# Six pairs of turned inputs put behind each other in a fused three-attention and MLP kernel

## The chip, the cores and the metric

The kernel runs on one core of a Trainium2 chip (trn2). The metric is the device time of one execution in microseconds (us); the figure for a kernel is the median of several executions. A profile is a separate, traced execution of the same program; it gives a span, from the first to the last instruction, and its own execution time beside it.

## The reference, cut to what matters

The input is `x` with 16 batches of 256 tokens and 256 features, and a context `y` of the same shape. Each batch goes through three attentions of 16 heads of 16 features, one after the other, and then through an MLP. All is float32.

```python
# layer 0: cross attention, RMS norms
q = rmsnorm(x) @ Wq;  k, v = rmsnorm(y) @ Wk, rmsnorm(y) @ Wv
x = rmsnorm(x + attention(q, k, v) @ Wo)
# layer 1: causal self attention with a layer norm ahead and rotary q and k
h = layernorm(x);  q, k, v = h @ sa_wq, h @ sa_wk, h @ sa_wv
x = x + causal_attention(rope(q), rope(k), v) @ sa_wo + sa_bo
# layer 2: cross attention with a layer norm ahead and rotary q and k
h = layernorm(x);  q = h @ ca_wq;  k, v = y @ ca_wk, y @ ca_wv
x = x + attention(rope(q), rope(k), v) @ ca_wo + ca_bo
# MLP
x = x + gelu(layernorm(x) @ fc1 + b1) @ fc2 + b2
```

The layers of one batch depend on each other. Different batches do not.

## The kernel before, in words

There are 48 attentions, three for each of 16 batches. Their order is written out by hand in the string `ORDER`, one digit for the layer of each; the n-th 0, the n-th 1 and the n-th 2 belong to batch n. The loop over `i` has 48 steps; step `i` does the scores and the values of attention `i`, and between them pieces of its neighbours. Within each engine the instructions stand in the order in which this loop names them; a manual schedule keeps it.

A step of layer 0 or layer 2 has four blocks `n` = 0 to 3. A step of layer 1, the causal one, has three, since one quarter of the scores is masked. In each block TensorE (PE in the profile) does scores (L472), values of the block before (L511), and then one dense product of 16 groups of rows:

- block 0: `q` of attention `i + 1` (L290)
- block 1: `k` of `i + 1` (L290)
- block `final - 1`: `v` of `i + 1` (L303); in a causal step this is block 1, so it follows `k` directly
- block `final`: the output projection `project` of `i - 2` (L303), and then the `turn` of `i + 2` (L270)

The turn makes the normalised input of an attention feature-major, since the products need it so. `turned` takes one PSUM bank, does four 128x128 transposes on TensorE (matmuls against the identity), and ScalarE (ACT) copies the bank to SBUF into a tile with the tag `hT` (L275). Attentions of layer 0 need no turn: their input is loaded in that layout already. So there are 32 turns.

What a turn needs is made by VectorE (DVE) and GpSimd (POOL) in two pieces. `stats` does `bn_stats` and `bn_aggr` for each half of the tokens (L252, L253), and then GpSimd adds epsilon (L234) and takes the power -1/2 (L235). `norm` waits for that and writes the normalised rows `xn`, one VectorE instruction for each half (L259). For attention `i + 2` both stand in step `i`, in block 0 or 1.

The rest of VectorE's queue matters for the steps below. After `q` and after `k` it does the rotary embedding (L402, L406, L422, L424 for `qm`, and L431, which writes `kT`). In block `final - 1` it inverts the softmax sums of `i - 1` (L553, L554), and adds the bias to `v` (L452, tile `va`), which releases the PSUM bank of `v`. In block `final` it adds the projected output to the rows (L576, in layer 0 L573 with two square sums L242). In block 0 of the next step it copies the values out of PSUM (L528, tile `av`). `divide` (L567) needs the inverted sums spread over partitions by a trip through DRAM (`inv<-hop`, issued by SP).

All dense products and the turns share three PSUM banks with the tag `d`, in rotation. Scores use two double banks, values one bank. The mask of a causal step is applied by GpSimd on the exponentials (L490). The scores of step `i` begin with `kT` and `qm` of attention `i`.

After the loop the MLP of eight groups of two batches follows, with its own turns (L657) and sums of inputs (`mix`). In the last step `mix` borrows two tiles of the tag `hT`.

Of the kernel before, what the change touches and what calls it, by code (L numbers as in the profile page):

```python
# [8 lines left out]
F32 = mybir.dt.float32  # L9
# [6 lines left out]
P = 128  # L16
B, S, D = 16, 256, 256
# [11 lines left out]
N_ATT = 3 * B  # L29

ORDER = [int(n) for n in "000001010102210210210121021012210101021212122222"]
# [14 lines left out]
def xattn_kernel(  # L46
# [25 lines left out]
    work = tc.alloc_tile_pool(name="work", bufs=2)  # L72
# [30 lines left out]
    def load(b):  # L103
        load_x(b)
        load_y(b)

    def load_w(t, aps, eng):
        at = 0
        for a in aps:
            m = a.shape[1]  # L110
            eng.dma_start(out=t[:, :, at : at + m], in_=a.rearrange("(k p) n -> p k n", p=P))
            at += m
# [41 lines left out]
    def dense_ps():  # L154
        return psD.tile([P, 512], F32, tag="d", name="d")
# [55 lines left out]
    def fold_v():  # L211
        ps = dense_ps()
        for k in range(KC):
            for j in range(0, P, 32):
                nc.tensor.matmul(
                    ps[j : j + 32, :D],
                    lhsT=vec[:, V_B1 + k : V_B1 + k + 1].to_broadcast([P, 32]),
                    rhs=sa_sb[:, k, 2 * D : 3 * D],
                    start=(k == 0), stop=(k == KC - 1), skip_group_check=True,
                )  # L220
        row = bias_sb[:, R_SAV : R_SAV + D]
        nc.vector.tensor_tensor(row, ps[:, :D], row, ALU.add)

    def fold_gain(w, cols, vcol, chunks=range(KC)):
        for k in chunks:
            nc.vector.tensor_scalar(
                w[:, k, cols], w[:, k, cols], vec[:, vcol + k : vcol + k + 1], None, ALU.mult
            )
# [36 lines left out]
    def turned(src, name, pool, tag, bufs):  # L265

        ps = dense_ps()
        for c in range(NC):
            for k in range(KC):
                nc.tensor.transpose(  # L270
                    ps[:, k * S + c * P : k * S + (c + 1) * P],
                    src[:, c, k * P : (k + 1) * P], ident,
                )
        t = pool.tile([P, KC, S], F32, tag=tag, name=name, bufs=bufs)
        nc.scalar.copy(t.rearrange("p k s -> p (k s)"), ps)  # L275
        return t
# [34 lines left out]
    class Att:  # L311
# [74 lines left out]
        def turn(self):  # L386
            if self.layer == 0:
                self.hT = xTs.pop(self.b)
            else:
                self.hT = turned(self.xn, "hT", work, "hT", 2)  # L390
            self.kvT = self.hT if self.layer == 1 else yTs[self.b]

        def rotated(self, ps, n):
# [192 lines left out]
    atts = {}  # L586

    def att(i):
        if 0 <= i < N_ATT:
            return atts.setdefault(i, Att(i))  # L590
        return None

    def do(i, *names):
        a = att(i)
        for name in names:
            if a is not None:
                getattr(a, name)()
# [37 lines left out]
    class Mlp:  # L635
# [24 lines left out]
                        )  # L660
                copy(self.hT[:, :, i, :], ps.rearrange("p (k s) -> p k s", s=S))

        def mix(self, tag="av"):

            b = self.hT
            if tag == "av":
                ts = self.pool.tile([P, 4, S], F32, tag=tag, name="ts")
                self.ts = [ts[:, i] for i in range(4)]
            else:
                pairs = [self.pool.tile([P, 2, S], F32, tag=tag, name="ts") for _ in range(2)]  # L670
                self.ts = [t[:, i] for t in pairs for i in range(2)]
            t1, t2, t3, t4 = self.ts
            for o, x, y in (
                (t1, b[:, 0, 1], b[:, 0, 0]), (t2, b[:, 1, 1], t1),
                (t3, b[:, 1, 1], b[:, 0, 1]), (t4, b[:, 1, 0], t2),
            ):
                nc.vector.tensor_tensor(o, x, y, ALU.subtract)
# [186 lines left out]
    mlps = [Mlp(g, work) for g in range(B // 2)]  # L864
    combined = combine()

    with tc.manual_schedule():
# [9 lines left out]
        load(3)  # L877
        load_w(sa_sb, sa, nc.sync)

        kept = {}  # L880
        for j in range(N_ATT):
            slot = next(i for i in range(max(j - 1, 0), N_ATT + 1) if (ORDER + [0])[i] != 1)
            kept.setdefault(slot, []).append(j)
        for i in range(N_ATT):
            a, last = att(i), att(i - 1)
            ahead = att(i + 3)
            if i > 1 and ahead is not None and ahead.layer == 0:
                load(ahead.b)

            finishing = i >= 3 and att(i - 3).layer == 0
            follows = (
                finishing and i + 2 < N_ATT
                and att(i + 2).layer == 1 and att(i + 2).b == att(i - 3).b
            )
            for n in range(len(a.blocks)):
                if n == 0 and a.causal and not finishing:
                    do(i + 2, "stats")
                a.scores(n)  # L900
                if n > 0:
                    a.values(n - 1)
                elif last is not None:
                    last.values(-1)
                final = len(a.blocks) - 1
                if n == 0:
                    if i == 0:
                        a.v()
                        do(1, "spread")
                    if not follows and (finishing or not a.causal):  # L910
                        do(i + 2, "stats")
                    do(i - 1, "end")
                    do(i - 3, "finish")
                    if follows:
                        do(i + 2, "stats")
                    if not finishing:
                        do(i + 2, "norm")
                    if i == N_ATT - 3:
                        mlps[0].stats()
                    if i == N_ATT - 2:  # L920
                        mlps[0].norm()
                    do(i - 2, "divide")
                    if i == N_ATT - 1:
                        mlps[0].turn(nc.vector.tensor_copy)
                        mlps[0].keep()
                    do(i + 1, "q")
                elif n == 1:
                    do(i + 1, "k")
                    if finishing:
                        do(i + 2, "norm")  # L930
                    for j in kept.get(i, ()):
                        att(j).keep()
                    if i == N_ATT - 1:
                        do(i - 2, "project")
                        mlps[1].norm()
                if n == final - 1:
                    do(i - 1, "invert")
                    do(i + 1, "v")
                    do(i + 2, "send")
                    if i == N_ATT - 2:  # L940
                        mlps[1].stats()
                    if i == N_ATT - 1:
                        mlps[0].up(2)
                        mlps[0].mix("hT")
                if n == final:
                    if i == N_ATT - 1:
                        mlps[1].turn(nc.vector.tensor_copy)
                    else:
                        do(i - 2, "project")
                    do(i + 2, "turn", "receive")  # L950
                if i == 0 and n == 0:
                    load(4)
                    nc.sync.dma_start(out=bias_sb, in_=rows.partition_broadcast(P))
                    nc.sync.dma_start(out=turn_sb, in_=turn)
                if i == 0 and n == 1:
                    load_w(ca_sb, ca, nc.sync)
                if i == 0 and n == 2:
                    load_w(fc1_sb, [fc1], nc.sync)
                if i == 1 and n == 0:
                    load_w(sao_sb, [sa_o], nc.sync)  # L960
                    load_w(cao_sb, [ca_o], nc.sync)
                if i == 1 and n == 2:
                    load_w(fc2_sb, [fc2], nc.sync)
                    nc.sync.dma_start(
                        out=rope_sb, in_=rope.rearrange("(c p) t d -> p c t d", p=P)
                    )
                if i == 1 and n == 3:
                    cols = fold_bias()
                    fold_v()
                if i == 2 and n == 3:  # L970
                    fold_gain(sa_sb, slice(0, 3 * D), V_G1)
                if i == 3 and n == 3:
                    fold_cols(cols)
                    fold_gain(ca_sb, slice(0, D), V_G2)
                if i in (6, 8) and n == 3:
                    fold_gain(fc1_sb, slice(0, FF), V_G3, [i // 8])
                if n == 1 and i > 8 and not a.causal:
                    next(combined, None)
# [72 lines left out]
    with tc.If(n_good < P):  # L1051
        with tc.tile_pool(name="gen", bufs=1) as gen, tc.tile_pool(
            name="gps", bufs=2, space=bass.MemoryType.PSUM
# [14 lines left out]
        with tc.tile_pool(name="late2", bufs=2) as late2, tc.tile_pool(  # L1068
            name="psL2", bufs=2, space=bass.MemoryType.PSUM
# [391 lines left out]
```

## Time and profile before

| what | value |
|---|---|
| median of 3 runs | 947.22 us (946.21 to 947.79) |
| profiled execution, own time | 945.63 us |
| profiled execution, span | 943.80 us |
| PE busy | 931.4 us, 99% of the span |
| DVE busy | 656.8 us, 70% |
| ACT busy | 546.8 us, 58% |
| POOL busy | 297.6 us, 32% |
| granted TensorE clock | 1.000 |

Of the 943.8 us, the first 60 load and begin, the stretch from 60 to 720 holds the steady part of the 48 steps, and the rest is the MLP. A matmul's row in the profile lasts longer than the distance to the next matmul, because matmuls are pipelined; so the time that a group of matmuls takes is read from the start of its first to the start of the next group, which is what the chain of work that ended last shows. Times in a timeline are counted from the start of the span.

### The profile page before, as it was taken

The page shows a single profiled execution, that of the slowest core. Times are in us where ns is not written, and L with a number is a line of the kernel's source. Part 1 is how long each engine was busy: PE and PEld are TensorE (multiplying, and loading weights), DVE is VectorE, ACT ScalarE, POOL GpSimd, SP SyncE. Part 2 cuts the span into 40 slices and gives each one's busy share as a digit, 9 for nine tenths or more (in the row PEclk, how much of TensorE's full clock was granted, in tenths as well). Part 3 has the DMA queues.
Part 4 walks back from the last instruction along what each step waited for, and adds up shares of the span by engine and source line. Part 5 has one row for each costly group of instructions (what it writes and reads, how often), then busy time and mean ns, then how long its engine had stood idle before and what let it go on. Part 6 is the DMA issues. An engine that isn't in the chain of part 4 may idle for free.

```text
span 943.8 us, 29943 instructions
## 1 busy us (share of the span) xinstructions
PE 931.4 (99%) x12374; PEld 550.1 (58%) x12374; DVE 656.8 (70%) x1438; ACT 546.8 (58%) x770; POOL 297.6 (32%) x501
## 2 busy tenths in 40 slices
PE   8999999999999999999999999999999999999997
PEld 3444455445454555455454554455444799999997
DVE  4348577876777677768766767888877576666663
ACT  3666556765666666756655666666666634444440
POOL 3122543424253454243423333344123021222200
PEclk9999999999999999999999999999999999999999
DMA  9541322213131131311232211111111100000001
GB/s 311 172 114 50 93 84 55 87 37 93 44 91 40 45 88 48 87 46 37 87 85 80 59 46 42 35 49 40 39 39 39 37 23 23 12 12 23 23 25 48
DMA packets 77994, 58.77 MB, mean 62 GB/s; under 512 B 25748, under 2 KB 76948, under 8 KB 77848
## 3 DMA queue, kind: packets, MB, share of 16 engines
q1 hardware_dynamic: 76616, 55.68, 20.7%
q8 instruction: 100, 1.64, 0.7%
q10 hardware_dynamic: 1232, 1.07, 0.4%
q14 instruction: 46, 0.38, 0.1%
HBM read 38.34 MB, written 5.79 MB: 47 GB/s over the span
## 4 chain that ended last, share of the span: by engine, by line
PE 87%; DMA 6%; DVE 4%; SPq 2%; issue 1%; POOL 0%; ACT 0%; ACTq 0%; DVEq 0%
PE S L472 17%; PE A L511 16%; PE d L303 15%; PE d L290 15%; PE upX L681 6%; PE A L779 5%; PE downZ L779 3%; PE upZ L681 3%; PE d L270 2%; PE d L779 2%; PE d L681 1%; DMA hop<-sums 1%; DMA sums<-hop 1%; DMA hop<-av 1%; DMA rq_hop<-pad 1%; PE d L657 1%
## 5 line engine op out<-in xcount | busy, mean ns | idle before, releaser
L483 ACT ACTIVATE pt<-S 128x1024 f32<-128x1024 f32 x224 | 217.3, 1022 | 121.0 <-PE S L472 121.0
L472 PE MATMUL S<-qm,kT 32*128 32x512 f32 (+1 forms) x1536 | 201.9, 600 | 1.0 <-ACT kT L433 0.7
L511 PE MATMUL A<-pt,va 128*32 128x256 f32 (+1 forms) x3072 | 188.9, 367 | 2.5 <-DVE av L528 2.5
L511 PEld LDWEIGHTS A<-pt,va 128*32 128x32 f32 x3072 | 80.2, 109 | 156.1 <-issue 106.3
L483 ACT ACTIVATE pt<-S,sy 128x1024 f32<-128x1024 f32 x128 | 135.7, 1111 | 47.5 <-PE S L472 45.1
L490 POOL TENSOR_SCALAR_AFFINE_SELECT pt<-pt 128x512 f32<-128x512 f32 x128 | 87.7, 702 | 61.3 <-ACT pt L483 60.8
L472 PEld LDWEIGHTS S<-qm,kT 32*128 32x128 f32 x1536 | 62.0, 183 | 66.6 <-issue 40.4
L398 ACT ACTIVATE a<-d,qk_bias 128x256 f32<-128x256 f32 x128 | 53.8, 471 | 53.8 <-PE d L290 43.9
L234 POOL TENSOR_SCALAR r_ln<-bmv 128x2 f32<-128x2 f32 x48 | 12.9, 268 | 224.4 <-DVE bmv L253 223.2
L279 POOL TENSOR_TENSOR cur<-cur,bias 128x512 f32<-128x512 f32 x48 | 64.2, 1343 | 55.5 <-DVE xn L259 55.5
L567 DVE TENSOR_TENSOR oT<-oT,inv 128x512 f32<-128x512 f32 x48 | 41.5, 864 | 30.5 <-DMA hop<-av 8.5
L290 PE MATMUL d<-hT,sa 128*32 128x256 f32 x1024 | 61.2, 379 | 0.0
L259 DVE TENSOR_SCALAR xn<-cur,bmv,r_ln 128x256 f32<-128x256 f32 x96 | 51.6, 585 | 1.4 <-POOL r_ln L235 0.8
L576 DVE TENSOR_TENSOR cur<-d,cur 128x512 f32<-128x512 f32 x32 | 22.0, 688 | 40.6 <-PE d L303 40.6
L406 DVE TENSOR_TENSOR a<-a,turn 128x512 f32<-128x512 f32 x64 | 48.1, 752 | 2.2
L417 DVE SCALAR_TENSOR_TENSOR qm<-d,vec,rq 128x512 f32<-128x512 f32 x32 | 22.5, 746 | 38.8 <-DMA rq<-rq_hop 36.1
L406 DVE TENSOR_TENSOR u<-u,turn 128x512 f32<-128x512 f32 x64 | 49.2, 768 | 0.0
L719 ACT ACTIVATE g<-g,fb 128x256 f32<-128x256 f32 x96 | 41.0, 499 | 11.1 <-DVE g L708 11.1
L528 DVE COPY av<-A 128x512 f32<-128x512 f32 x47 | 32.2, 684 | 21.8 <-PE A L511 21.8
L402 DVE STREAM_SHUFFLE u<-a 128x512 f32<-128x512 f32 x64 | 47.3, 739 | 0.0
L290 PEld LDWEIGHTS d<-hT,sa 128*32 128x32 f32 x1024 | 33.4, 110 | 21.9 <-ACT pt L483 0.3
L234 POOL TENSOR_SCALAR r_o<-ms_o 128x2 f32<-128x2 f32 x16 | 5.1, 322 | 128.9 <-DVE sq L242 117.0
(149 smaller groups left out, 1571.0 us busy)
## 6 DMA issues: line engine op xcount, KB each, us to landing
oT<-av SPq DMA_DIRECT2D x384, 32.0 KB
inv<-hop SPq DMA_DIRECT2D x96, 128.0 KB
cur<-in_x SPq DMA_DIRECT2D x16, 256.0 KB
xT<-in_xt SPq DMA_DIRECT2D x16, 256.0 KB
yT<-in_yt SPq DMA_DIRECT2D x16, 256.0 KB
y<-in_y SPq DMA_DIRECT2D x16, 256.0 KB
out<-res SPq DMA_DIRECT2D x15, 256.0 KB
fc<-in_fc SPq DMA_DIRECT2D x2, 1024.0 KB
```

What stands on the lines that cost most here:

```text
L259: nc.vector.tensor_scalar(xn[:, c, :], src[:, c, :], mv[:, c, 0:1], r[:, c : c + 1], ALU.subtract, ALU.mult,)
L279: nc.gpsimd.tensor_tensor(t, t, bias_sb[:, row : row + D].unsqueeze(1).to_broadcast([P, NC, D]), ALU.add)
L290: nc.tensor.matmul(ps[j : j + 32, t * S : (t + 1) * S], lhsT=w[:, k, at + t * P + j : at + t * P + j + 32], rhs=src[:, k, :], start=(k == ...
L303: nc.tensor.matmul(ps[j : j + 32, c * D : (c + 1) * D], lhsT=src[:, k, c * P + j : c * P + j + 32], rhs=w[:, k, at : at + D], start=(k == ...
L398: nc.scalar.activation(a[:, t], ps[:, t], AF.Identity, bias=bias[:, t : t + 1])
L406: nc.vector.tensor_tensor(t, t, table.unsqueeze(1).to_broadcast([P, KC, S]), ALU.mult)
L472: nc.tensor.matmul(ps[:, j, 2 * m * u : 2 * m * (u + 1)] .rearrange("p (i s) -> p i s", i=2), lhsT=self.kT[r, t, kc * P : (kc + 1) * P], r ...
L483: nc.scalar.activation(pt[:, :, :w], ps[:, :, :w], AF.Exp, scale=scale)
L490: nc.gpsimd.affine_select(out=diag, in_=diag, compare_op=ALU.is_ge, fill=0.0, base=0, pattern=[[0, 2], [0, 2], [1, P]], channel_multiplier=-1,
L511: nc.tensor.matmul(self.av[32 * r : 32 * r + 32, i, q0:S], lhsT=self.va[:, kc, 8 * t + 2 * r + i, :], rhs=pts[r // 2][:, r % 2, i * m : (i ...
L681: nc.tensor.matmul(banks[c // 2][:, (c % 2) * S : (c % 2 + 1) * S], lhsT=a[:, c * P : (c + 1) * P], rhs=b, start=(first and c % 2 == 0), s ...
L779: nc.tensor.matmul(ps[:, c, :], lhsT=a[f // 2][:, f % 2, c * P : (c + 1) * P], rhs=b[:, f, :], start=(first and c == 0 and f == 0), stop=True,
```

## The change

The set `paired` is worked out from `ORDER`. It has six members, the attentions 13, 23, 30, 39, 42 and 44. For each member `j`, `stats` and `norm` move from step `j - 2` to step `j - 3`, into block `final - 1` behind `invert` and `v`, and its turn moves to the end of step `j - 3`, directly behind the turn of `j - 1`. The six steps with two turns are 10, 20, 27, 36, 39 and 41, all of layer 0 or 2; the six steps that lose theirs are 11, 21, 28, 37, 40 and 42. Of these 21, 28, 40 and 42 are causal, 11 and 37 are not. Tiles with the tag `hT` get three buffers where they had two, also in the last `mix`.

```diff
-                self.hT = turned(self.xn, "hT", work, "hT", 2)
+                self.hT = turned(self.xn, "hT", work, "hT", 3)
...
+        paired = set()
+        for i in range(3, N_ATT - 5):
+            j = i + 3
+            if ORDER[i] != 1 and min(ORDER[i + 2], ORDER[j]) > 0 and i + 2 not in paired:
+                b = ORDER[:j].count(ORDER[j])
+                p = [q for q in range(j) if ORDER[q] == ORDER[j] - 1][b]
+                if p + 6 <= j:
+                    paired.add(j)
...
             for n in range(len(a.blocks)):
+                due = i + 2 if i + 2 not in paired else None
                 if n == 0 and a.causal and not finishing:
-                    do(i + 2, "stats")
+                    do(due, "stats")
...
                     if not finishing:
-                        do(i + 2, "norm")
+                        do(due, "norm")
...
                     do(i - 1, "invert")
                     do(i + 1, "v")
                     do(i + 2, "send")
+                    if i + 3 in paired:
+                        do(i + 3, "stats", "norm")
...
                         do(i - 2, "project")
-                    do(i + 2, "turn", "receive")
+                    do(due, "turn", "receive")
+                    if i + 3 in paired:
+                        do(i + 3, "turn")
```

The other calls of `stats` and `norm` for `i + 2` take `due` in the same way, `do` does nothing for `None`, and the last `mix` names three buffers for its two `hT` tiles.

More of the change, by code (lines that the diff above doesn't have):

```diff
@@ L588, in att @@
     def att(i):
-        if 0 <= i < N_ATT:
+        if i is not None and 0 <= i < N_ATT:
             return atts.setdefault(i, Att(i))
@@ L661, in turn, with mix @@
                 copy(self.hT[:, :, i, :], ps.rearrange("p (k s) -> p k s", s=S))
-        def mix(self, tag="av"):
+        def mix(self, tag="av", bufs=None):
             b = self.hT
@@ L669, in mix @@
             else:
-                pairs = [self.pool.tile([P, 2, S], F32, tag=tag, name="ts") for _ in range(2)]
+                pairs = [
+                    self.pool.tile([P, 2, S], F32, tag=tag, name="ts", bufs=bufs)
+                    for _ in range(2)
+                ]
                 self.ts = [t[:, i] for t in pairs for i in range(2)]
@@ L910, in xattn_kernel @@
                     if not follows and (finishing or not a.causal):
-                        do(i + 2, "stats")
+                        do(due, "stats")
                     do(i - 1, "end")
@@ L914, in xattn_kernel @@
                     if follows:
-                        do(i + 2, "stats")
+                        do(due, "stats")
                     if not finishing:
-                        do(i + 2, "norm")
+                        do(due, "norm")
                     if i == N_ATT - 3:
@@ L929, in xattn_kernel @@
                     if finishing:
-                        do(i + 2, "norm")
+                        do(due, "norm")
                     for j in kept.get(i, ()):
@@ L943, in xattn_kernel @@
                         mlps[0].up(2)
-                        mlps[0].mix("hT")
+                        mlps[0].mix("hT", 3)
                 if n == final:
```

## The prediction

> **What bounds the kernel now.** I read the busy time and the chain of the profile page first, then the chain in order of time around turns, then the timeline of all engines around the six steps that get a second turn.
>
> ```profile
> PE 931.4 (99%) x12374; PEld 550.1 (58%) x12374; DVE 656.8 (70%) x1438; ACT 546.8 (58%) x770; POOL 297.6 (32%) x501
> ...
> PE 87%; DMA 6%; DVE 4%; SPq 2%; issue 1%; POOL 0%; ACT 0%; ACTq 0%; DVEq 0%
> ```
>
> TensorE is the bound: 99% busy and 87% of the chain. In the steady part nothing else carries the chain, so any time that PE loses there is lost in full, and any that it saves is saved. Next the chain in order of time, in two stretches (columns: start, time until the next piece, piece).
>
> ```profile
> 610.27 1.73 PE d L303 x32
> 612.00 0.59 PE d L270 x4
> 612.59 1.07 PE S L472 x8
> ...
> 719.44 1.00 PE A L511 x16
> 720.44 1.02 PE d L657 x8
> 721.47 1.19 PE S L472 x8
> ```
>
> A turn of four transposes costs PE 0.59 us. Eight transposes in one place, at the start of the MLP, cost 1.02, between neighbours of the same kinds. So a pair costs 2 x 0.59 - 1.02 = 0.16 us less than two single turns, if its inputs are there. Whether they are is read from the timeline of step 39 and the end of step 40 (columns: start, duration, instruction, idle time before it).
>
> ```profile
> 611.10 0.63 DVE L452 TENSOR_TENSOR va<-d,bias 128x512 f32<-128x512 f32 x1
> ...
> 611.93 0.66 PE L270 MATMUL d<-ident,xn 128*128 128x128 f32 x4
> 612.07 0.69 DVE L576 TENSOR_TENSOR cur<-d,cur 128x512 f32<-128x512 f32 x1 [0.34 <-PE d L303]
> 612.51 1.14 PE L472 MATMUL S<-qm,kT 32*128 32x512 f32 x8
> ...
> 612.67 0.42 DVE L252 BATCH_NORM_STATS2 bst<-cur 128x6 f32<-128x256 f32 x1
> ...
> 613.92 0.22 POOL L234 TENSOR_SCALAR r_ln<-bmv 128x2 f32<-128x2 f32 x1 [10.46 <-DVE bmv L253]
> 614.23 0.71 POOL L235 TENSOR_TENSOR r_ln<-r_ln,nhalf 128x2 f32<-128x2 f32 x1
> ...
> 615.33 0.73 DVE L259 TENSOR_SCALAR xn<-cur,bmv,r_ln 128x256 f32<-128x256 f32 x2
> ...
> 624.44 1.01 DVE L431 TENSOR_TENSOR kT<-a,u 128x512 f32<-128x512 f32 x1
> ...
> 625.23 0.66 PE L270 MATMUL d<-ident,xn 128*128 128x128 f32 x4
> ```
>
> The change puts L252 to L259 directly behind L452. Here L452 starts only 0.83 us before the turn, while the way from L252 to the end of L259 is about 3 us. And at the end of the causal step the turn starts at 625.23, while `kT`, which the scores after it need, is ready at 625.45.
>
> **What the Trainium skill says.** "TensorEngine Tiling (Array Packing)", Key Properties: "Mode switching requires drain". The trace agrees: 128x128 transposes stand between 128x32 projections and 32x128 scores, and a pair saves one way in and out, 0.16 us. "PSUM — Partial Sum Buffer", Engine vs sequencer instructions, says that VectorE's queue is strict FIFO; so a waiting L259 holds up all behind it. The trace agrees: rows of one engine keep the program's order. "SBUF — State Buffer", Who interferes with whom, says that only the port pair of VectorE and GpSimd causes contention. The trace fits: L431 takes 0.69 us mostly, and 1.01 at 624.44 beside the mask L490.
>
> **The change part by part.** *On PE.* Six turns leave: 6 x 0.59 = 3.54 us less. Six second turns add 0.43 each (1.02 - 0.59) if they are on time, and more if `xn` is late.
>
> *The moved norm.* After L452 starts, the next VectorE instruction begins 0.54 later (0.63 less 0.09 overlap, as from L576 to L252, 0.69 and 0.60). From L252 to the end of L235 it is 612.67 to 614.94, 2.27 us, a round trip through POOL, which was idle for 10 us or more at all six places. L259 follows after 0.04 and takes 0.73 for both halves. So `xn` is complete 3.58 us after the start of L452. The third transpose needs its second half; a matmul waiting on VectorE starts 0.05 after it (L528 ends at 112.35, L511 starts at 112.40), the fourth follows 0.11 later and the scores 0.20 after that. So the scores cannot start before L452 + 3.94. I compare that with the start of the scores in the trace of before; the later of it and the on-time 0.43 counts:
>
> - step 10: 178.49 + 3.94 = 182.43 against 181.97: +0.46
> - step 20: 329.04 + 3.94 = 332.98 against 331.88: +1.10
> - step 27: 431.90 + 3.94 = 435.84 against 435.04: +0.80
> - step 36: 563.03 + 3.94 = 566.97 against 567.22: on time, +0.43
> - step 39: 611.10 + 3.94 = 615.04 against 612.51: +2.53
> - step 41: 638.99 + 3.94 = 642.93 against 642.03: +0.90
>
> The sum is 6.22. Step 39 is the worst since VectorE runs late there: `divide` waits 2.34 us for `inv<-hop` at 603.05, and from then on VectorE has hardly a gap up to L452. Nothing of that moves in the change.
>
> *Where the turns leave.* At steps 11 and 37 `kT` is ready more than 3 us ahead, and the 0.59 is gained whole. At the causal steps 21, 28, 40 and 42 `kT` ends 0.21 to 0.22 us after the place where the scores would now start (344.81 against 344.60, 447.97 against 447.75, 625.44 against 625.23, 654.96 against 654.75). The stats and the norm that leave these steps do not make it earlier: L402, which begins the chain to `kT`, waits for ACT's biased copy of `q` (L398; 0.23 us idle ahead of L402 at 336.70, 439.86 and 646.85), which waits for PE. With 0.05 to 0.14 for waking PE (L511 starts at 81.64, 0.14 after L528 ends, where a wait instruction stands between), I take 0.31 each: 4 x 0.31 = 1.24 back. Then step 41 begins 0.28 earlier on PE, but its VectorE chain starts from `divide` at 630.99, which waits for a DMA; so its second turn is 0.28 later still.
>
> *What lies beside other work.* The second ACT copy (0.59) ends about 0.7 after the turns, and ACT's next exponential waits 1.1 us for scores in any case; without that cover it would cost up to 0.59 a place, which I leave at nothing. VectorE's L573/L576, L242 and L528 now queue behind L259. L576 frees the PSUM bank that the next `q` takes; it would end at L452 + 4.27, and that `q` starts 1.96 after the scores, at L452 + 5.90, so 1.6 us of margin hide it. The second turn takes the bank of `v`, which L452 itself has freed. POOL's two instructions move into idle time. SP issues the same DMAs in the same order. The third `hT` buffer and `mix` cost no time that I can find: the buffer spares the second copy a wait at best; bounds 0.0 to 0.2 us.
>
> **The sum:** -3.54 + 6.22 + 1.24 + 0.28 = +4.2 us. Against the profiled execution's 945.63 this is 949.8; that execution lay 1.6 below the median of 947.22, so for the median I say **951.4**. The unknown sizes are VectorE's start at each place (it shifts each of five late turns by perhaps 0.2 either way) and the wait for `kT` (0.2 to 0.4): together about +2.8 to +6.
>
> **Rivals.** *In time after all*: VectorE is idle 0.3 to 3.1 us ahead of L573/L576 at these places, and if the moved 3 us fitted into it every pair would cost 0.43. The point is where L452 starts 2.92 us ahead of the first turn (3.94 less 0.59 less 0.43); the trace has 2.90, 2.26, 2.55, 3.60, 0.83 and 2.46. For it: steps 10 and 36 fit. Against it: step 39 lacks 2.1. It would give 6 x 0.43 - 3.54 + 1.24 = +0.3, 947.5, not slower; with no wait for `kT` either -0.96, 946.3. *Late norm, but no wait for kT*: if the chain to `kT` gets shorter with the lighter VectorE, +2.7, 949.9. Against it speaks that this chain is released by ACT. *A knock-on*: the late L576 and L528 hold up `q` or values in the next step, or the earlier causal steps run into further waits; another 0.5 us at each of six places gives +7.2, 954.4. For it: VectorE already runs late around step 39; against it the 1.6 us of margin. That the second turns do not stand together is excluded by the program's order, in which eight transposes follow each other six times.
>
> **How the numbers follow.** My case has 0.60, in time after all 0.12, no wait for `kT` 0.14, the knock-on 0.14. About 0.2%, 1.9 us, is what a measurement of this kernel can tell from no change: below 945.3 would be faster, above 949.1 slower. My case lies above 949.1 with nearly all of its chance, the knock-on wholly, the case without the `kT` wait mostly; in time after all counts as no change with a little of it faster. That makes 0.03 faster, 0.16 within, 0.81 slower. The range 948.0 to 954.8 takes in my case with its bounds and a spread of runs of about 1 us, the third case and about half of the knock-on.
>
> **What would show it.** In the new profile the pairs should appear as eight transposes; at steps 10 and 36 PE should pass through them in about 1.02 us; at step 39 PE should stand still for about 2 us between the fourth and the fifth transpose, waiting for `xn` L259, and at 20, 27 and 41 for 0.4 to 0.9. The scores that open steps 22, 29, 41 and 43 should wait for `kT` L431 by about 0.3. PE's waits on VectorE should grow by some 5 us in all. I am wrong if the eight transposes run without a gap at step 39, if the waits on L431 are missing, or if PE waits at L290 or L511 in the steps after a pair.

## The result, and the profile after

| | before | after |
|---|---|---|
| median, 7 runs each on one chip | 947.59 us (946.21 to 949.47) | 954.27 us (949.94 to 955.48) |
| ratio | | 1.0072, 95% interval 1.0058 to 1.0086 |
| profiled execution, own time | 945.63 us | 953.18 us |
| its span | 943.80 us | 951.4 us |

The change makes the kernel slower by 0.72%: 6.8 us of 947.6, between 5.5 and 8.1. The forecast for the median was 951.4 with a range to 954.8, and 0.81 on slower. The sign was right; the median came 2.9 us above the forecast, and the loss is 6.8 us where 4.2 were forecast. Of the seven executions after, five had a granted TensorE clock of 0.997 or 0.998 and took 953.1 to 955.5 us, and the two at 0.999 and 1.000 took 953.2 and 949.9; what this has to do with the change comes up again below.

First the page of the kernel after: busy time, and the chain that ended last by engine.

```profile
PE 932.7 (98%) x12374; PEld 550.4 (58%) x12374; DVE 657.0 (69%) x1438; ACT 546.4 (57%) x770; POOL 295.6 (31%) x501
...
PE 70%; DVE 12%; DMA 9%; SPq 4%; issue 2%; POOL 1%; ACT 1%; ACTq 0%; DVEq 0%
```

No engine got more work: counts are the same, and busy times nearly so. But TensorE's share of the chain fell from 87% to 70%, and VectorE's rose from 4% to 12%: the end of the program now hangs on pieces of VectorE, and on DMAs, which rose from 6% to 9%. What TensorE waited for is in its list of waits (us in total, times, longest):

```profile
PE d L270 <- DVE xn L259: 3.8, 5, 2.1
...
PE S L472 <- ACT av L528: 1.2, 4, 0.3
```

The five waits of a turn on the normalised rows stand at steps 20, 27, 36, 39 and 41. Four of them were forecast, with about 2 us as the longest, at step 39; the one at step 36 was not. (At step 10 the wait is too short for the list.) The second row is the four waits of 0.3 after the four causal steps; the name in it is not the cause, as the run without the mask shows below.

Step 39 in the timeline of the kernel after (columns: start, duration, instruction, idle time before it):

```profile
615.41 0.63 DVE L452 TENSOR_TENSOR va<-d,bias 128x512 f32<-128x512 f32 x1
615.95 0.42 DVE L252 BATCH_NORM_STATS2 bst<-cur 128x6 f32<-128x256 f32 x1
616.06 0.66 PE L270 MATMUL d<-ident,xn 128*128 128x128 f32 x4
...
617.20 0.22 POOL L234 TENSOR_SCALAR r_ln<-bmv 128x2 f32<-128x2 f32 x1 [9.39 <-DVE bmv L253]
617.50 0.71 POOL L235 TENSOR_TENSOR r_ln<-r_ln,nhalf 128x2 f32<-128x2 f32 x1
618.25 0.74 DVE L259 TENSOR_SCALAR xn<-cur,bmv,r_ln 128x256 f32<-128x256 f32 x2 [1.13 <-POOL r_ln L235]
618.81 0.67 PE L270 MATMUL d<-ident,xn 128*128 128x128 f32 x4 [2.09 <-DVE xn L259]
...
619.41 1.14 PE L472 MATMUL S<-qm,kT 32*128 32x512 f32 x8
```

The first turn starts 0.65 us after L452. The second turn's rows first go from VectorE to GpSimd and back, and TensorE stands still for 2.09 us between the fourth and the fifth transpose. From L452 to the scores it is 4.00 us, where the forecast had 3.94.

A place is the end of a step, where a second turn was added or the only turn left. Its cost is read from TensorE's timeline: the time from the start of the projection ahead of the turns to the start of the scores behind them, less the same time in the kernel before. For the kernel after, and a second execution of it on another chip:

| place | forecast | after | second execution |
|---|---|---|---|
| step 10, pair | +0.46 | +0.52 | +0.52 |
| step 20, pair | +1.10 | +1.15 | +1.15 |
| step 27, pair | +0.80 | +0.86 | +0.86 |
| step 36, pair | +0.43 | +1.17 | +1.66 |
| step 39, pair | +2.53 | +2.76 | +2.78 |
| step 41, pair | +0.90 + 0.28 | +1.20 | +1.17 |
| steps 11 and 37, leaving | -0.59 each | -0.59 each | -0.59 each |
| steps 21, 28, 40, 42, leaving | -0.28 each | -0.22 to -0.23 | -0.22 to -0.27 |
| sum | +4.2 | +5.6 | +6.0 |

The whole profile of after ends 7.6 us later than that of before. The other 2.1 us lie outside these places: 1.5 in the first 165 us, and 0.5 in step 33, where the projection waits 0.36 us for VectorE. These stretches differ by more between executions of one kernel: the second execution of the kernel after is 1.9 us quicker outside the places than the kernel before. From 165 us to the end, TensorE waits nowhere for more than 0.15 us but in step 33 and at the places, and from step 43 on nothing is added or lost.

One number rules the late places: the lead of L452, from its start to the start of the first turn. The scores start 4.00 us after L452, the first turn takes 0.59, and so a pair costs 4.00 - 0.59 less the lead, or 0.43 if that is more. At step 39 the lead is 0.65 in the kernel after, which gives 2.76; at step 36 it is 2.24 and 1.75 in the two executions, which gives 1.17 and 1.66.

### The profile page after: what moved, and what is told of

Same layout as the page of the kernel before. It is cut to its first block, busy times and chain, and to the rows that moved or that the text cites. A ratio compares the mean times of both kernels' runs of the same rounds, so it can differ in the third digit from the quotient of the medians.

```text
span 951.4 us, 29938 instructions
## 1 busy us (share of the span) xinstructions
PE 932.7 (98%) x12374; PEld 550.4 (58%) x12374; DVE 657.0 (69%) x1438; ACT 546.4 (57%) x770; POOL 295.6 (31%) x501
## 3 DMA queue, kind: packets, MB, share of 16 engines
q8 instruction: 100, 1.64, 0.7%
## 4 chain that ended last, share of the span: by engine, by line
PE 70%; DVE 12%; DMA 9%; SPq 4%; issue 2%; POOL 1%; ACT 1%; ACTq 0%; DVEq 0%
PE S L472 13%; PE A L511 12%; PE d L290 11%; PE d L303 10%; PE upX L684 6%; PE A L782 5%; PE downZ L782 3%; PE upZ L684 3%; DMA hop<-av 2%; SPq L544 2%; DMA hop<-sums 2%; DVE u L402 2%; PE d L782 2%; DMA inv<-hop 1%; DVE a L406 1%
## 5 line engine op out<-in xcount | busy, mean ns | idle before, releaser
L490 POOL TENSOR_SCALAR_AFFINE_SELECT pt<-pt 128x512 f32<-128x512 f32 x128 | 87.9, 704 | 75.7 <-ACT pt L483 75.5
L279 POOL TENSOR_TENSOR cur<-cur,bias 128x512 f32<-128x512 f32 x48 | 63.7, 1333 | 55.5 <-DVE xn L259 55.5
L567 DVE TENSOR_TENSOR oT<-oT,inv 128x512 f32<-128x512 f32 x48 | 38.7, 807 | 38.5 <-DMA inv<-hop 16.5
L259 DVE TENSOR_SCALAR xn<-cur,bmv,r_ln 128x256 f32<-128x256 f32 x96 | 52.9, 600 | 8.6 <-POOL r_ln L235 7.6
L406 DVE TENSOR_TENSOR u<-u,turn 128x512 f32<-128x512 f32 x64 | 50.3, 786 | 0.0
L406 DVE TENSOR_TENSOR a<-a,turn 128x512 f32<-128x512 f32 x64 | 46.1, 720 | 2.2
L777 DVE TENSOR_TENSOR g<-g,g 128x512 f32<-128x512 f32 x64 | 40.9, 682 | 0.0
```

Source lines behind the costliest of these rows:

```text
L279: nc.gpsimd.tensor_tensor(t, t, bias_sb[:, row : row + D].unsqueeze(1).to_broadcast([P, NC, D]), ALU.add)
L406: nc.vector.tensor_tensor(t, t, table.unsqueeze(1).to_broadcast([P, KC, S]), ALU.mult)
L490: nc.gpsimd.affine_select(out=diag, in_=diag, compare_op=ALU.is_ge, fill=0.0, base=0, pattern=[[0, 2], [0, 2], [1, P]], channel_multiplier=-1,
```

## The experiments

Times are compared with runs of the kernel before on the same chip: median 945.57 for the first four, 945.43 for the next four, 945.89 for the three after them, 946.54 for the last.

**The kernels themselves, on one chip.** The first two runs are the kernels before and after, unedited.

> The kernel before, unchanged, for a second profile. Theory (the time is lost in PE's waits for the moved norm at the six pairs, 7.7 us, less 2.1 us where turns left): groups of matmuls around the six places take the same time in both profiles of the kernel before, within 0.1 us; differences between the two profiles lie elsewhere, mostly in the first 200 us, and add up to about 2 us. The DMA inv<-hop lands up to 1.5 us later or earlier from one execution to the next, so VectorE's start at single places differs by as much, without any cost on PE. Rival (the 2 us that the changed kernel's profile shows outside the six places belong to the change): the second profile of the kernel before agrees with the first within 0.5 us there.

> The changed kernel, unchanged, for a second profile. Theory: steps 10, 20, 27, 39 and 41 again show scores late by 0.52, 1.15, 0.86, 2.76 and 1.20 us within 0.2; step 36, whose VectorE chain waited 1.64 us for the DMA inv<-hop in the first profile and 0.21 in the kernel before, shows anything between 0.43 (DMA early) and 1.2 us (DMA late), following that wait one for one. Rival (step 36 is late because of the change itself): again 1.17 us there, whatever the DMA did.

Measured: 945.55 and 949.63 us in one execution each. The second is the last column of the table above. In the kernel before, `divide` (L567) of attention 34, ahead of step 36, waited 1.69 us for `inv<-hop` here and 0.21 in the first profile, and the lead of L452 in step 36 was 2.07 us here and 3.60 there. So that wait belongs to the execution and not to the change. It cost the kernel before nothing, since a single turn needs no result of VectorE's that late: its places take the same time in both profiles, within 0.01 us. Outside the places the two profiles of the kernel before agree in sum, as the rival said, but only because 0.9 us less in the first 165 us stands against 0.9 more in steps 33 to 35. The two of the kernel after differ there by 4.0, so these stretches say nothing of the change.

**The third bank alone.**

```diff
-                self.hT = turned(self.xn, "hT", work, "hT", 2)
+                self.hT = turned(self.xn, "hT", work, "hT", 3)
...
```

The last `mix` names three buffers too.

> The kernel before with the third buffer of the tag hT alone, no pairs. Theory: no difference, 0.0 us within the interval, since no wait on hT stands on PE's chain. Rival (the larger pool moves other buffers or delays the last step): +1 us or more.

Measured: 945.40 us, ratio 0.9992 (0.9981 to 1.0004). The bank costs nothing that can be measured.

**The worst pair alone.**

```diff
-                if p + 6 <= j:
+                if p + 6 <= j and j in (42,):
```

> The change with one pair alone, attention 42 turned at the end of step 39, the five others as before. Theory: +2.76 us at step 39 less 0.23 at step 40, +2.5 us in all (ratio 1.0027), plus up to 0.3 where step 41 then starts earlier against its DMA, which costs nothing without a second turn there. Rival (the loss is a general one of six pairs, spread evenly): a sixth of 6.7 us, +1.1 us.

Measured: 949.1 us, ratio 1.0035 (1.0023 to 1.0047), so +3.3 us (2.2 to 4.4), which excludes an even share. In its profile step 39 costs +2.55 and step 40 gives -0.23, together +2.3. One pair of six thus carries about two fifths of what the places lose. The 1.0 us between the runs and the places goes with the clock: 11 of its 20 executions had a granted clock of 0.999 or 1.000 and a median of 947.8 us, which is +2.2, and nine had 0.997 or 0.998 and a median of 950.2. The kernel before shows 0.998 once in 83 executions on three chips and never less.

**The stats early, the norm still behind `v`.** The comment is not in the kernel; it says where the line stands.

```diff
...
+                    if i + 3 in paired:
+                        do(i + 3, "stats")      # block 0
...
-                        do(i + 3, "stats", "norm")
+                        do(i + 3, "norm")
```

> The changed kernel with only the stats of the second turn moved from behind v to block 0 of the same step; the norm stays behind v. So VectorE no longer waits there for POOL's two instructions. Theory (the wait is the round trip through POOL): the scores can start 1.7 us after L452 where they started 4.0 after it, which is in time at steps 10, 20, 27, 36 and 41 (+0.43 each) and about in time at step 39 (+0.4 to +0.8); the four causal steps still give back 0.23 each only, and 11 and 37 give 0.59. Sum 6 x 0.43 to +2.9, less 2.10: +0.5 to +0.9 us against the kernel before, so 5.8 to 6.2 us faster than the changed kernel. Rival (turns behind each other are slow of themselves, or the PSUM bank of v holds the second one up): still +4 us or more.

The result stands behind the next version.

**Stats and norm both early.** To the edit above comes that the second norm stands in block 1, ahead of `v`.

```diff
+                    if i + 3 in paired:
+                        do(i + 3, "norm")       # block 1
...
-                    if i + 3 in paired:
-                        do(i + 3, "norm")
```

> The changed kernel with stats of the second turn in block 0 and its norm in block 1 of the same step, so that the input of the second turn is ready long before it. Theory: every pair costs PE 1.02 us, 6 x 0.43 less 2.10 is +0.5 us against the kernel before; at step 39, where VectorE is late, v's L452 comes 0.65 later, and the second turn, which takes the bank that L452 frees, may wait up to 0.4 us. PE shows no wait on L259 at the pairs. Rival: the same as for stats early; or the 0.65 us of L259 ahead of q's and k's work makes kT late in these steps and costs more than +2 us.

Measured: 949.39 us, ratio 1.0037 (1.0023 to 1.0051), for the first of the two versions, and 949.1 us, ratio 1.0038 (1.0025 to 1.0051), for the second. Both were expected within 1 us of the kernel before, and both miss that: about half of the loss stayed. With the round trip out of the way, steps 10, 27, 36 and 41 are on time at +0.43 to +0.44 in both, as expected. Steps 20 and 39 are not: +0.80 and +1.84 in the first, +1.02 and +2.04 in the second. (In the first, step 40 lost 0.21, and in the second, step 21 lost 0.10, where the causal steps gain 0.23 otherwise; both times `kT` is late. That was not followed up.) The timeline of the first version at step 39:

```profile
614.66 0.63 DVE L452 TENSOR_TENSOR va<-d,bias 128x512 f32<-128x512 f32 x1
615.20 0.72 DVE L259 TENSOR_SCALAR xn<-cur,bmv,r_ln 128x256 f32<-128x256 f32 x2
...
615.75 0.67 PE L270 MATMUL d<-ident,xn 128*128 128x128 f32 x4 [0.78 <-DVE xn L259]
```

From L452 to the scores it is now 1.69 us, as forecast. But the work that was moved stands ahead of L452 and makes it late itself: the lead of L452 fell from 2.26 us to 0.31 at step 20, and at step 39 from 0.65 to less than nothing, 0.45 behind the start of the first turn. The expectation had left this out. The second version at step 39:

```profile
614.22 1.38 DVE L259 TENSOR_SCALAR xn<-cur,bmv,r_ln 128x256 f32<-128x256 f32 x4
...
615.52 0.35 DVE L554 RECIPROCAL sums<-sums 128x32 f32<-128x32 f32 x1
615.78 0.63 DVE L452 TENSOR_TENSOR va<-d,bias 128x512 f32<-128x512 f32 x1
...
616.46 0.66 PE L270 MATMUL d<-ident,xn 128*128 128x128 f32 x4 [1.01 <-DVE va L452]
```

The rows `xn` of both turns are ready early (x4, 1.38 us), and now TensorE waits for something else. The second turn takes the PSUM bank of `v`, which L452 frees, and L452 stands behind the four L259. The moved norm was put ahead of the very instruction that the second turn needs. From L452 to the scores it is 1.27 us here, but the lead fell by another 0.65, the time of the moved norm, at steps 20 and 39. The wait for `xn` has become a wait for a bank, with a late VectorE behind both, and part of its lateness is the moved work.

**Two pairs, early.** The version above with members 13 and 39 only (places 10 and 36, whose leaving steps are not causal).

```diff
-                if p + 6 <= j:
+                if p + 6 <= j and j in (13, 39):
```

> Stats and norm early as in e4, and only the two pairs whose turns leave a step that is not causal (attentions 13 and 39). Theory: 2 x (0.43 - 0.59) = -0.3 us, which a measurement cannot tell from nothing; in the profile the two pairs show +0.43 and the two steps -0.59. Rival (the saving of a pair is not real on the chip): the pairs show +0.59.

Measured: 945.82 us, ratio 1.0001 (0.9990 to 1.0012). The places show +0.44 and +0.43, the leaving steps -0.59 each: 0.3 us won in the profile, too little for the runs to tell from no change.

**The mask off.** The causal mask on GpSimd (L490) runs beside VectorE's L431, which writes `kT`.

```diff
-                if self.causal:
+                if False:
                     # the mask, L490
```

> The changed kernel without GpSimd's mask of the causal steps (L490), which leaves that part of the computation out. Without it VectorE does not share its port pair with GpSimd in the causal steps. Theory (the 0.36 us of the gain that is lost at steps 21, 28, 40 and 42 is the wait for kT, late through that sharing): in the profile these four steps now give the whole 0.59 us instead of 0.23, and kT's L431 takes 0.69 us there and not 1.01. Rival (scores wait there for ACT's copy of the values, L528, or for the bank of scores): still 0.23.

Measured: 947.99 us in one execution. Here are the last instruction of the chain to `kT`, ACT's `av` that the list of waits names, and the scores, first from the kernel after at the end of step 40:

```profile
631.34 1.00 DVE L431 TENSOR_TENSOR kT<-a,u 128x512 f32<-128x512 f32 x1
...
631.79 0.60 ACT L528 COPY av<-A 128x512 f32<-128x512 f32 x1
...
632.49 1.14 PE L472 MATMUL S<-qm,kT 32*128 32x512 f32 x8 [0.29 <-ACT av L528]
```

and then from the version without the mask:

```profile
625.78 0.69 DVE L431 TENSOR_TENSOR kT<-a,u 128x512 f32<-128x512 f32 x1
...
627.43 0.59 ACT L528 COPY av<-A 128x512 f32<-128x512 f32 x1
...
627.76 1.14 PE L472 MATMUL S<-qm,kT 32*128 32x512 f32 x8
```

With the mask L431 takes 1.00 us and ends at 632.34, and the scores start 0.15 later. Without it L431 takes 0.69 and ends 1.3 us ahead of the scores, which start without idle time of TensorE. All four causal steps then give the whole 0.59. `av` ends almost together with `kT` in the kernel after, at 632.39, so the list cannot tell the two apart. Without the mask the scores start 0.26 ahead of the end of `av`, and so they do not wait for it. The bank of scores is no rival either: the exponentials that free it end 0.57 us ahead of the scores in the kernel after, and 0.2 ahead of them without the mask. So the four waits of 0.3 that the list puts down to ACT's `av` are waits for `kT`.

**Without the DMA behind `divide`.** Two instructions L567 no longer need the inverted sums.

```diff
-            nc.vector.tensor_tensor(self.oT, self.oT, self.inv, ALU.mult)
+            by = turn_sb.rearrange("p (t s) -> p t s", t=KC) if self.i in (34, 37) else self.inv
+            nc.vector.tensor_tensor(self.oT, self.oT, by, ALU.mult)
```

> The changed kernel, in which the divide of attentions 34 and 37 (VectorE's L567, in steps 36 and 39) multiplies by a resident tile instead of the inverted sums; so two attentions lack their division, and these two instructions no longer wait for inv<-hop (in the changed kernel they stood idle 1.6 to 1.9 us and 2.4 us). Theory A (the second turn is late by as much as VectorE is late with v's bias L452, and in steps 36 and 39 that lateness is the DMA behind divide): step 36 costs +0.44 instead of +1.17 and +1.66, and step 39 between +0.5 and +1.2, as steps 10, 20, 27 and 41 do, instead of +2.76; the longest wait of TensorE on L259 falls from 2.1 to under 0.9; one execution about 2.5 to 3.5 us below the changed kernel, so 946.5 to 948. Theory B (step 39 is late for another reason, the round trip through GpSimd or VectorE's own work ahead of L452): step 39 stays at +2.3 or more, and the time at 949 or above.

Measured: 953.03 us in one execution. Step 36 costs +0.43, as the first theory said. Step 39 costs +1.74, which neither said. The time lies on the second theory's side, but does not decide: the places add up to +3.8, and the rest lies in the first 165 us and in steps 33 to 35, which the edit does not touch. Why only 1.0 of step 39 was saved is seen in VectorE's timeline ahead of it, and GpSimd's beside it:

```profile
605.87 0.81 DVE L568 TENSOR_TENSOR oT<-oT,turn 128x512 f32<-128x512 f32 x1
...
607.41 0.97 DVE L406 TENSOR_TENSOR a<-a,turn 128x512 f32<-128x512 f32 x1
608.30 1.77 DVE L406 TENSOR_TENSOR u<-u,turn 128x512 f32<-128x512 f32 x1
```

```profile
606.09 3.42 POOL L279 TENSOR_TENSOR cur<-cur,bias 128x512 f32<-128x512 f32 x2
```

`divide` (here L568) no longer waits. VectorE is early, and runs into GpSimd's two bias additions L279, which in the kernel after took 2.51 us and ended 0.25 us after VectorE had started again. Two L406 take 0.97 and 1.77 us instead of 0.69: 1.37 us lost again. The lead of L452 is 1.67 us.

**The same with the early norm.**

> The version with stats and norm of all six moved ahead of v (stats in block 0, norm in block 1), with the same two divides not waiting for inv<-hop (attentions 34 and 37 lack their division). Without that edit step 39 cost +2.04, since L452 frees the bank for the second turn only after four L259 on a late VectorE. Theory A (VectorE late from the DMA): step 39 falls to +0.44, all sites but step 20 (+1.0, no edit there) are on time; the sum of the six pairs is about 3.2, of the leaving turns -1.9 to -2.1. Theory B (VectorE's own work of the block, 1.4 us of L259, is what makes it late): step 39 stays above +1.2.

Measured: 949.46 us in one execution; step 39 +1.42 (from +2.04), step 20 +1.01, the other pairs on time. The number lies on the second theory's side, but not for its reason alone: L279 stands beside the early VectorE here as well, an L406 took 1.75 and L422 1.66.

**And without GpSimd's additions in step 39.** To the edit of `divide` in the kernel after comes:

```diff
-            if self.layer > 0:
+            if self.layer > 0 and self.i not in kept[39]:
                 add_bias(self.x, R_SAO if self.layer == 1 else R_CAO)
```

> The changed kernel with the two divides of attentions 34 and 37 not waiting for inv<-hop (as in the run before this one of that kind), and in step 39 also without GpSimd's two bias additions L279 (3.42 us in all, for attentions 39 and 40, whose output bias is left out). With the divides alone step 39 fell only from +2.76 to +1.74; there VectorE worked without a gap from its stats to L452, and two L406 that ran beside L279 took 0.97 and 1.77 us instead of 0.69. Theory A (the earlier VectorE runs into GpSimd's L279 at their shared port and loses 1.37 us): both L406 take 0.69 to 0.71, L452 starts about 1.4 us earlier against TensorE, and step 39 costs +0.44 to +0.6. Theory B (the slow L406 have another cause, or something else ahead of L452, such as ACT's copy of q, becomes the wait): step 39 stays at +1.0 or more. The time of one execution alone does not decide: 945 to 952.

Measured: step 39 costs +0.52 (one execution, 951.12 us). Timelines of VectorE and of TensorE at step 39:

```profile
606.69 0.69 DVE L406 TENSOR_TENSOR a<-a,turn 128x512 f32<-128x512 f32 x1
607.30 0.68 DVE L406 TENSOR_TENSOR u<-u,turn 128x512 f32<-128x512 f32 x1
...
613.34 0.63 DVE L452 TENSOR_TENSOR va<-d,bias 128x512 f32<-128x512 f32 x1
```

```profile
616.24 1.17 PE L270 MATMUL d<-ident,xn 128*128 128x128 f32 x8
617.34 1.14 PE L472 MATMUL S<-qm,kT 32*128 32x512 f32 x8
```

Both L406 are at 0.69, L452 leads the turn by 2.90 us where it led by 0.65 in the kernel after, and the eight transposes pass in 1.10 us. So the whole excess of step 39 is VectorE's lateness, and that has two layers: the DMA behind `divide`, and under it VectorE and GpSimd slowing each other. That they meet at a shared port was argued in the prediction; the runs show the slowdown and whose work causes it, not the port.

**Four pairs, early.** Members 13, 30, 39 and 44: steps 20 and 39 keep their single turns.

> Stats and norm early as before (stats in block 0, norm in block 1), but only four pairs: members 13, 30, 39 and 44, so that the steps 20 and 39, where this order was late, keep their single turns. Theory A (what is left of the loss in the early versions, ratio 1.0037, lies at steps 20 and 39 alone): pairs 4 x 0.44 = 1.75, leaving turns -0.59 - 0.25 - 0.59 - 0.23 = -1.66, so +0.1 us and a ratio of 1.000, between 0.9988 and 1.0012. Theory B (moved norms cost VectorE time elsewhere, which the places do not show): ratio 1.002 or more. No version of this kind can gain more than the 0.16 us for each pair whose leaving step gives the whole 0.59.

Measured: 945.76 us, ratio 1.0003 (0.9992 to 1.0013). Places +0.44 four times, leaving steps -0.59, -0.25, -0.59, -0.23: +0.1 us. What the early versions lost lay in steps 20 and 39. No version tried beats the kernel before.

## Why the prediction was right, and where it was off

- **What bounds the kernel.** Right. TensorE is the bound, and each wait at the places went into the time.
- **A pair saves 0.16.** Right. On-time pairs cost +0.43 or +0.44 in every version. That the change of tiling mode is the reason was argued and not tried.
- **The late norm behind L452.** The mechanism held at steps 10, 20, 27, 39 and 41. Steps 10, 20 and 27 cost 0.05 to 0.06 more, since the path from L452 to the scores takes 4.00 us and not 3.94; step 39 cost 0.23 more, 0.06 for the path and the rest for a lead of 0.65 us where it had been 0.83. Together +0.4. That steps 20 and 39 came out so near is in part luck: the lead at step 20 was 2.26 us in the first profile of the kernel before and 1.31 in the second, which would have cost +2.10, and at step 39 it was 1.76 in the profile of the third bank alone.
- **Step 36 on time at +0.43.** This term failed: +1.17 and +1.66. I took L452's lead of 3.60 us there from one profile as fixed; after, it was 2.24 and 1.75. It hangs on `divide` of attention 34, and the DMA behind it lands when it lands. The rows of L567, first from the profile before, then from the two executions after:

```profile
555.71 0.69 DVE L567 TENSOR_TENSOR oT<-oT,inv 128x512 f32<-128x512 f32 x1 [0.21 <-DMA inv<-hop]
```

```profile
560.66 0.69 DVE L567 TENSOR_TENSOR oT<-oT,inv 128x512 f32<-128x512 f32 x1 [1.64 <-DMA inv<-hop]
```

```profile
557.15 0.69 DVE L567 TENSOR_TENSOR oT<-oT,inv 128x512 f32<-128x512 f32 x1 [1.94 <-DMA inv<-hop]
```

  With the wait gone step 36 was at +0.43, and the lead at 3.60. The lead without a late DMA was right; that it would be there was the error, worth 0.7 to 1.2 us, the largest of the sum.
- **The wait for `kT`.** Right in kind, as the run without the mask shows. My sign of being wrong, that waits on L431 are missing, did appear in the list of waits by name, and is answered there. The size was 0.36 and not 0.31 for each causal step, since waking TensorE took 0.15 us, just past the upper end of my bounds: +0.2.
- **Step 41 later by what step 40 gives.** The number is right, +1.20 and +1.17 against +1.18, and the lead fell from 2.46 to 2.22. The reason is shown only in part: in the second profile of the kernel before the lead is already 2.33.
- **The bank and the second copy at nothing.** The bank: right, ratio 0.9992. The copy was not tried by itself; the on-time pairs leave no room for a cost on TensorE.
- **The rivals.** Neither the bank nor the `q` behind a pair made TensorE wait, so the loss near the 954.4 of the knock-on did not come from a knock-on. In time after all is excluded by step 39, no wait for `kT` by the four waits.

With these corrections the sum of 4.2 becomes 5.6, which is what the places of the first profile add up to; the second execution has 6.0. The runs say 6.8 (5.5 to 8.1). The range took in 6.8 only because it reached into the knock-on, which did not come; the bounds of my own case ended at +6, so that the measured time lies in the range owes something to luck. What the rest of about 1 us is stays open. It can be chance, or the first 165 us, which differ so much. The clock is a third candidate: 0.997 or 0.998 was granted in five of seven executions after and in nine of twenty with the pair at step 39 alone, where these took 2.4 us longer, but in four of the other 66 executions of versions without a standstill of 2 us, and once in 83 of the kernel before. Both of the former let TensorE stand still for about 2 us at step 39. Whether that lowers the clock is not shown: none of the executions at 0.997 was traced, and the traced ones keep the full clock up to their last 3 us.

One cause I had not carried far enough: I named the late `divide` for step 39, but not what would follow if it came in time. The version with the norm early shows that a better place for the norm does not mend it, and the three runs on the divide show that behind one cause of VectorE's lateness there was a second.

## What to carry to other kernels

Saving on the bounding engine is worth only what its inputs leave: here 0.16 us for a pair stood against 0.1 to 2.3 us of waiting, and where the leaving step already waited for something else, the 0.59 it gave fell to 0.23. Before moving work to an earlier place, read the lead of the slowest input there, in more than one execution if a DMA stands in its chain, and count what the moved work itself adds to the queue there: moved further ahead, it took 2.6 us off the lead at step 20. And ask of each wait that is taken away what the engine will then run into: a wait for `xn` became a wait for a bank, a wait for a DMA became a slowdown beside another engine.

## What the hardware showed that was not expected

- The way of the inverted sums back from DRAM took 3.94, 5.39 and 4.88 us, from the first issue of `inv<-hop` to `divide` of attention 34, in three executions (before, after, after again), and its issue moved as well; VectorE's wait for it was 0.21 and 1.69 us in two executions of the kernel before and 1.64 and 1.94 in two of the kernel after.
- A 128x512 VectorE multiplication that takes 0.69 us took 0.97 to 1.77 beside GpSimd's addition of two tiles, and these two additions took 3.42 us where they had taken 2.51 with VectorE idle. Each engine slowed the other.
- In the list of waits, a wait on two semaphores was put down to ACT's `av` in four cases; it ended 0.05 us after `kT` in the one shown, and only taking away the mask, which let the scores start ahead of `av`, showed the wait to be for `kT`.
